# Row gathers that add in place into six accumulators, and a lasting buffer for edge offsets

## The chip, the cores and the metric

The kernel runs on one core of a Trainium2 chip. The metric is the device time of one execution in microseconds (us), as the median of several runs; lower is better. Besides the times there is one execution taken by the hardware profiler. The engines are called as the profile calls them: PE (TensorE, matmuls), DVE (VectorE), ACT (ScalarE), POOL (GpSimd, which asks for the gathers) and SP (SyncE, which asks for the plain transfers).

## The reference

A graph network with 6250 nodes, 256 channels, 100,000 edges sorted by destination, three layers and a head. Cut to what matters:

```
N, E, C, NOUT, NL = 6250, 100000, 256, 64, 4
h = relu(layernorm(x));  y = h
def agg(y): return segment_sum(y[src], dst, num_segments=N)
for l in range(NL - 1):
    t = relu((y + agg(y)) @ W1s[l] + b1s[l])
    t = relu(t @ W2s[l] + b2s[l])
    y = t @ W3s[l] + b3s[l]
t = relu((y + agg(y)) @ cW1 + cb1)
t = relu(t @ cW2 + cb2)
return x + t @ cW3 + cb3
```

All arrays are float32. Each node has some 16 incoming edges, so `agg` sums some 16 rows of 256 values per node, four times over.

## The kernel before, in words

**Blocks and two ways to aggregate.** The 6250 nodes are 49 blocks of 128. Since matrix products commute with the sum over edges, each layer's table holds rows that are multiplied by the layer's first weights already, and the aggregation works on these. Most blocks are aggregated on PE: a matrix of edge counts (uint8) is built once from one-hot tiles, kept in DRAM, and multiplied in every layer with the table, which lies in SBUF as a high and a low part (`XY`). These are the `panels`; a product step is line 1565, its operand `a` is a cast of a uint8 chunk by ACT or DVE (lines 1538 and 1540).

**Gathered blocks.** The blocks in `gone` are aggregated from rows instead (`Gathered`, lines 1341 to 1484): 22 blocks in layer 0 and 18 in each of the three others, 76 in all. For each block POOL issues 19 indirect DMAs, each of 128 rows of 1 KB, one row for each node of the block: `K` = 17 take the first 17 edges of every node (`idx`), `OV` = 2 take the block's further edges (`over`), which a small matmul with a one-hot (`hot`) sums into the right nodes. In the kernel before, the first 16 rows come in pairs into tiles `rows` of [128, 2, 256], seven of them in turn; row 17 and the two overflow gathers have tiles `last`. `pair` (lines 1413 to 1419) adds each pair of rows on DVE into `acc` as soon as it is due; `fold` (line 1421) adds the table's own rows, both halves of `acc` and row 17 into `u`, and then makes `hot`; `add` (line 1442) runs the overflow matmuls `sums` on PE; `finish` adds them into `u`, transposes and goes on to the layer's matmuls.

**What sets the order.** Everything runs under an order written out by hand: PE's stream of matmuls advances a clock (`passed`, line 1515), and the gathers of a layer are spread evenly over it. `begin` (line 1370) sets the layer's `first` and `pace`; `flow` and `send` (lines 1375 to 1398) issue each gather `LEAD` = 13 clock us ahead of its event, bound to the last matmul so far by a semaphore (`after`). `advance` runs `pair`, `fold` and `add` when their event is due, whether the rows have landed or not: an engine then waits in order at that instruction.

**Preparation.** Before the matrix is built, the edges of each block are found (`look`, from line 612): `from_i` (line 816) holds for each of the 128 nodes of the 22 gathered blocks where its run of edges begins, and 22 gathers on POOL (line 606, asked for in line 821) take 17 sources from there for each node into `idx`. `from_i` is in the preparation's pool. When that pool is closed, the build's tiles, `pairs` (line 1061) first, are laid over its memory. At build step `READY` = 22 (line 1607) `slot_rows` (line 850) masks `idx` on DVE, and layer 0's gathers begin. A build step is two one-hot matmuls (line 1108) and the cast of their result; steps run two at a time before the first product.

Of the kernel before, what the change touches and what calls it, by code (L numbers as in the profile page):

```python
# [8 lines left out]
F32 = mybir.dt.float32  # L9
I32 = mybir.dt.int32  # L10
# [4 lines left out]
OP = mybir.AluOpType  # L15
PSUM = bass.MemoryType.PSUM
DRAM = bass.MemoryType.DRAM
P = 128
# [378 lines left out]
def sorted_edges(  # L397
# [38 lines left out]
    nc = tc.nc  # L436
    N, C = x.shape
# [16 lines left out]
    K, OV = 17, 2  # L454
    SLOT = K + OV
# [14 lines left out]
    NG = sum(n for _, n in gone)  # L470
# [4 lines left out]
    const = ctx.enter_context(tc.tile_pool(name="const", bufs=1))  # L475
# [11 lines left out]
    live = const.tile([P, NG, K], F32, name="live")  # L487
    nodes3 = const.tile([P, 3, NG], F32, name="nodes3")
    gained = const.tile([P, NG], F32, name="gained")
    taken = const.tile([P, NG, 2], BF16, name="taken")  # L490
    slots = const.tile([P, OV * P], BF16, name="slots")
    kth = const.tile([P, K], F32, name="kth")
# [2 lines left out]
    colf = const.tile([P, P], F32, name="colf")  # L495
# [116 lines left out]
    def look(pool):  # L612
# [29 lines left out]
        half = pool.tile([P, 2], F32, name="half", bufs=1)  # L642
# [170 lines left out]

        st, dg = nodes3[:, 0, :], nodes3[:, 1, :]
        at0 = pool.tile([P, NG], F32, name="at0", bufs=1)
        from_i = pool.tile([P, NG], I32, name="from_i", bufs=1)
        nc.vector.tensor_scalar(at0, st, float(E - K), None, op0=OP.min)
        nc.vector.tensor_copy(from_i, at0)
        for c in range(NG):
# [177 lines left out]
    with tc.manual_schedule():  # L997
# [55 lines left out]
        hot = {}  # L1053
# [3 lines left out]
        def pair(hots, k):  # L1057

            if k < len(batches):
                s = batches[k][1]  # L1060
                pairs[s] = hots.tile([P, 2, GSUB, 2], BF16, name="pairs", bufs=3)
                nc.scalar.copy(pairs[s], clT[:, :, :, s, None].to_broadcast([P, 2, GSUB, 2]))  # L1062
# [172 lines left out]
        def bring_inputs(b0, n):  # L1235

            assert layers[NLAYER].sent == len(layers[NLAYER].order)
            assert layers[NLAYER].done == layers[NLAYER].n
            inputs[b0] = []
            for _ in range(0, n, 2):  # L1240
                t = gath.tile([P, 2, C], F32, name="rows", bufs=7)
                inputs[b0].extend((t[:, 0, :], t[:, 1, :]))
            for i, t in enumerate(inputs[b0]):
                rows_io(x, b0 + i, 1, t[:, None, :], True)
# [96 lines left out]
        class Gathered:  # L1341
            def __init__(self, l):
                self.l, self.sent, self.done = l, 0, 0
                self.first, self.turn = None, None
                self.blocks = [(b, n, i, left[q] + i)
                               for q, (b, n) in enumerate(gone) for i in range(n)
                               if l == 0 or (b, n) != panels[-1]]
                self.alone = {b + i for b, n, i, _ in self.blocks}
                self.rows, self.us, self.acc, self.hot = {}, [], None, None
                self.order = [(g, k) for g in range(len(self.blocks)) for k in range(SLOT)]  # L1350
                self.events = []
                for g in range(len(self.blocks)):
                    for k in range(3, K - 1, 2):
                        self.events.append((SLOT * g + k, lambda g=g, k=k: self.pair(g, k)))
                    self.events.append((SLOT * g + K - 1, lambda g=g: self.fold(g)))
                    self.events.append((SLOT * g + SLOT - 1, lambda g=g: self.add(g)))
                self.n = len(self.events)
# [22 lines left out]
            def send(self, upto):  # L1380
                while self.sent < min(upto, len(self.order)):
                    g, k = self.order[self.sent]
                    c = self.blocks[g][3]
                    if k < K - 1:
                        if k % 2 == 0:
                            self.rows[g, k + 1] = gath.tile([P, 2, C], F32, name="rows", bufs=7)
                        t = self.rows[g, k | 1][:, k % 2, :]
                    else:
                        t = self.rows[g, k] = gath.tile([P, C], F32, name="last", bufs=4)
                    at = idx[:, c, k:k + 1] if k < K else over[:, c, k - K:k - K + 1]  # L1390
                    got = nc.gpsimd.indirect_dma_start(  # L1391
                        out=t, out_offset=None, in_=tables[self.l][:, :],
                        in_offset=bass.IndirectOffsetOnAxis(ap=at, axis=0),
                    )
                    after(got, "rows are asked for evenly over a layer")
                    self.sent += 1
                    if self.l == 0 and k == 4 and g + 2 < len(self.blocks):
                        ahead.append(self.blocks[g + 2][3])
# [11 lines left out]
                    self.done += 1  # L1410
                    run()

            def pair(self, g, k):
                t = self.rows.pop((g, k))
                if k == 3:
                    self.acc = work.tile([P, 2, C], F32, name="acc", bufs=1)
                    nc.vector.tensor_tensor(self.acc, self.rows.pop((g, 1)), t, OP.add)
                else:
                    nc.vector.tensor_tensor(self.acc, self.acc, t, OP.add)  # L1419

            def fold(self, g):
                if self.turn in jobs:
                    jobs.remove(self.turn)
                    self.turn[2]()
                b, n, i, c = self.blocks[g]
                b += i
                u = work.tile([P, C], F32, name="u", bufs=2)
                self.us.append(u)
                nc.vector.tensor_tensor(u, XY[:, b, :C].bitcast(F32), XY[:, b, C:].bitcast(F32),  # L1429
                                        OP.add)  # L1430
                used.add((self.l, b, 0))
                if (self.l, b, 1) in used:
                    used.add((self.l, b))
                    reload(self.l, b)
                nc.vector.tensor_tensor(u, u, self.acc[:, 0, :], OP.add)  # L1435
                nc.vector.tensor_tensor(u, u, self.acc[:, 1, :], OP.add)  # L1436
                nc.vector.tensor_tensor(u, u, self.rows.pop((g, K - 1)), OP.add)
                self.hot = work.tile([P, OV, P], F32, name="hot", bufs=2)
                nc.vector.tensor_tensor(self.hot, colf[:, None, :].to_broadcast([P, OV, P]),  # L1439
                                        rel[:, c, :, None].to_broadcast([P, OV, P]), OP.is_equal)  # L1440

            def add(self, g):
                b, n, i, _ = self.blocks[g]
                for j in range(OV):
                    mm = nc.tensor.matmul(sums[:, :C], self.hot[:, j, :], self.rows.pop((g, K + j)),  # L1445
                                          start=(j == 0), stop=(j == OV - 1))
                    passed(C * FULL32, mm)
                self.finish(b, n, i, sums)
# [42 lines left out]
        units = [(0, -1, j) for j in range(PRE)] + [  # L1491
            (l, p, j) for l in range(NLAYER + 1) for p in range(last[l] + 1) for j in range(NT)]
        sums = ps_g.tile([P, W], F32, name="sums")
        LEAD, TAIL = 13.0, 10.0
        COLS, FULL32, TURN, BUILD, BURST = 0.457e-3, 1.68e-3, 0.4, 0.2, 0.3
        clock = [0.0]
        FAR, SPAN = 7, 6
# [101 lines left out]
        with tc.tile_pool(name="hots", bufs=1) as hots, tc.tile_pool(  # L1599
            name="ats", bufs=1  # L1600
        ) as ats, tc.tile_pool(name="rings", bufs=AHEAD + 2) as rings, tc.tile_pool(
            name="gath", bufs=1
        ) as gath, tc.tile_pool(
            name="ps_a", bufs=2, space=PSUM
        ) as ps_a, tc.tile_pool(name="ps_b", bufs=2, space=PSUM) as ps_b:
            begun = {0: clock[0]}
            READY = 22
            spread = {u: [] for u in range(2, 2 * PRE + 1, 2)}
            spread[READY - 4], spread[READY - 2] = [layers[0].blocks[0][3]], [
                layers[0].blocks[1][3]]  # L1610
            beside = build(hots, ats, ps_b)
            while now[0] < PRE:
                for _ in range(2):
                    next(beside)
                    built[0] += 1
                if built[0] == READY:
                    slot_rows()
                    layers[0].begin()
                for c in spread[built[0]]:
                    overflow(hots, c)  # L1620
                tick(layers[0])
                layers[0].advance()
                if built[0] == GSUB * (panels[0][1] - 1) + 4:
                    open_chunks()
            later(1, lambda: later(2, lambda bad=verdict(): judge(bad)))
            for p in range(last[0] + 1):
                product(0, p, ps_a, beside)
            assert next(beside, None) is None and built[0] == total
# [72 lines left out]
```

## Time and profile before

| what | value |
|---|---|
| median of 3 runs | 2530.39 us (2521.58 to 2542.65) |
| profiled execution | 2534.08 us, its span 2532.2 us |
| mean granted PE clock | 0.923 of full speed |
| DVE busy in pairwise adds, first and further (lines 1417, 1419) | 52.2 and 313.0 us |
| indirect DMAs on POOL, L1391 | 1216 of `rows`, 76 + 152 of `last` |
| DMA engines' mean share over the layers | 0.49 to 0.52 |

The profile gives, for each engine, the time that its instructions took, and for each group of instructions the idle time ahead of it with what ended it (`<-`). A line `A <- B: t, n, m` of the waits says that A's engine stood idle n times for t us in all, at most m us in one piece, until B was done. In a timeline row stand the start, the duration, the engine, the line, the operation with out<-in and shapes, and in brackets the idle time before it.

### The profile page before, as it was taken

The page shows a single profiled execution, that of the slowest core. Times are in us where ns is not written, and L with a number is a line of the kernel's source. Part 1 is how long each engine was busy: PE and PEld are TensorE (multiplying, and loading weights), DVE is VectorE, ACT ScalarE, POOL GpSimd, SP SyncE. Part 2 cuts the span into 40 slices and gives each one's busy share as a digit, 9 for nine tenths or more (in the row PEclk, how much of TensorE's full clock was granted, in tenths as well). Part 3 has the DMA queues.
Part 4 walks back from the last instruction along what each step waited for, and adds up shares of the span by engine and source line. Part 5 has one row for each costly group of instructions (what it writes and reads, how often), then busy time and mean ns, then how long its engine had stood idle before and what let it go on. Part 6 is the DMA issues. An engine that isn't in the chain of part 4 may idle for free. (4 is left out here: it accounts for less than half of the span.)

```text
span 2532.2 us, 29316 instructions
## 1 busy us (share of the span) xinstructions
PE 2149.9 (85%) x9093; PEld 1603.5 (63%) x9093; DVE 1315.5 (52%) x2939; ACT 896.4 (35%) x1812; POOL 1588.1 (63%) x1574
## 2 busy tenths in 40 slices
PE   5848878777787899989989899899898989888888
PEld 3726655555555687666667686666666866666665
DVE  6758666666666644444334553344334544444344
ACT  4745453434444443222223432222223422222222
POOL 3356666666666537767667367676667276777673
PEclk9959998988898899999999999999999999899898
DMA  5425545444445555444545455445445545554553
GB/s 154 137 85 168 161 136 153 148 143 150 151 136 174 171 168 150 148 148 136 157 143 155 145 178 154 148 139 157 141 156 157 166 152 166 158 160 145 169 156 106
DMA packets 201369, 381.40 MB, mean 151 GB/s; under 512 B 35538, under 2 KB 126050, under 8 KB 201204
## 3 DMA queue, kind: packets, MB, share of 16 engines
q0 software_dynamic: 72768, 192.26, 25.9%
q1 hardware_dynamic: 126510, 185.34, 22.6%
q10 hardware_dynamic: 1926, 1.85, 0.3%
q8 instruction: 73, 1.20, 0.2%
q14 instruction: 92, 0.75, 0.1%
HBM read 320.38 MB, written 58.59 MB: 150 GB/s over the span
## 5 line engine op out<-in xcount | busy, mean ns | idle before, releaser
L1565 PE MATMUL agg<-a,XY 128*128 128x512 f32 (+1 forms) x6076 | 1612.1, 415 | 121.7 <-issue 74.8
L1391 POOL DMA_INDIRECT rows<-table,idx x1216 | 1237.7, 1018 | 681.8 <-issue 220.6
L1565 PEld LDWEIGHTS agg<-a,XY 128*128 128x128 f32 x6076 | 1173.2, 200 | 418.3 <-issue 136.4
L1538 ACT CAST a<-at 128x512 fp32r<-128x512 uint8 (+1 forms) x943 | 546.3, 606 | 769.0 <-PE agg L1565 464.3
L1540 DVE CAST a<-at 128x512 fp32r<-128x512 uint8 (+1 forms) x576 | 260.3, 461 | 443.4 <-PE agg L1565 229.6
L1419 DVE TENSOR_TENSOR acc<-acc,rows 128x512 f32<-128x512 f32 x456 | 313.0, 686 | 34.2 <-DMA rows<-table,idx 23.1
L1108 PE MATMUL bp<-hi,lo 128*128 128x196 bf16 x992 | 154.9, 272 | 139.8 <-issue 49.3
L1116 ACT CAST at<-bp 128x392 uint8<-128x392 f32 x276 | 131.4, 486 | 356.3 <-PE bp L1108 157.5
L1118 DVE CAST at<-bp 128x392 uint8<-128x392 f32 x220 | 123.9, 563 | 196.1 <-PE bp L1108 98.7
L1108 PEld LDWEIGHTS <-lo 128*128 128x128 bf16 x992 | 84.9, 104 | 219.1 <-issue 155.8
L1391 POOL DMA_INDIRECT last<-table,over x152 | 159.6, 1050 | 75.4 <-issue 25.4
L1260 PE MATMUL ps<-h,w 128*128 128x512 f32 (+5 forms) x392 | 162.3, 554 | 2.2 <-issue 2.0
L1289 PE MATMUL ps<-w,h 128*128 128x256 f32 x588 | 142.2, 388 | 17.7 <-ACT h L1473 6.3
L1067 DVE TENSOR_TENSOR hi<-cols,pairs 128x784 bf16<-128x784 bf16 x248 | 139.3, 562 | 0.0
L1289 PEld LDWEIGHTS ps<-w,h 128*128 128x128 f32 x588 | 112.8, 194 | 41.3 <-issue 17.3
L1455 DVE TENSOR_TENSOR u<-u,sums 128x256 f32<-128x256 f32 x76 | 31.8, 418 | 202.3 <-PE agg L1565 161.7
L1067 DVE TENSOR_TENSOR lo<-lanes,pairs 128x512 bf16<-128x512 bf16 x248 | 104.1, 420 | 26.1 <-ACT pairs L1062 23.1
L1260 PEld LDWEIGHTS ps<-h,w 128*128 128x128 f32 (+1 forms) x392 | 68.8, 189 | 69.9 <-issue 60.6
L1445 PE MATMUL sums<-last,hot 128*128 128x256 f32 x304 | 85.7, 405 | 27.7 <-DVE hot L1439 18.1
L1263 ACT ACTIVATE h<-ps,bias 128x512 f32<-128x512 f32 (+5 forms) x98 | 60.5, 634 | 133.8 <-PE agg L1565 56.6
L1391 POOL DMA_INDIRECT last<-table,idx x76 | 80.8, 1063 | 38.6 <-issue 13.8
L1307 DVE TENSOR_TENSOR zz<-ps,w 128x512 f32<-128x512 f32 (+1 forms) x78 | 50.1, 657 | 93.7 <-PE agg L1565 36.3
(167 smaller groups left out, 1110.5 us busy)
## 6 DMA issues: line engine op xcount, KB each, us to landing
at<-mat SPq DMA_DIRECT2D x189, 448.0 KB
mat<-at SPq DMA_DIRECT2D x31, 784.0 KB
rows<-table,idx POOLq DMA_INDIRECT x1216
table<-zz SPq DMA_DIRECT2D x69, 256.0 KB
back<-table SPq DMA_DIRECT2D x118, 128.0 KB
at<-mat SPq DMA_DIRECT2D x25, 336.0 KB
xs<-in_x_dram SPq DMA_DIRECT2D x8, 768.0 KB
table<-zs SPq DMA_DIRECT2D x24, 256.0 KB
```

Of the source, the lines that this page charges most:

```text
L1067: nc.vector.tensor_tensor(o.rearrange("p q (n t) -> p q n t", t=2), values.rearrange("p (n t) -> p n t", t=2)[:, None, :, :].to_broadcast( ...
L1108: mm = nc.tensor.matmul(bp[:, m * HW:(m + 1) * HW], lo[:, q + m, :], hi[:, q + m, :], start=True, stop=True)
L1116: nc.scalar.copy(o, v)
L1118: nc.vector.tensor_copy(o, v)
L1260: mm = nc.tensor.matmul(ps[:mp, :w], weights[l][0][:, c, i * P:i * P + mp], h1[:, c, :w], start=(c == 0), stop=(c == KC - 1))
L1289: mm = nc.tensor.matmul(o, h2[0][:, c, nodes], w3[:, c, :], start=(c == 0), stop=(c == KC - 1))
L1391: got = nc.gpsimd.indirect_dma_start(out=t, out_offset=None, in_=tables[self.l][:, :], in_offset=bass.IndirectOffsetOnAxis(ap=at, axis=0),)
L1419: nc.vector.tensor_tensor(self.acc, self.acc, t, OP.add)
L1445: mm = nc.tensor.matmul(sums[:, :C], self.hot[:, j, :], self.rows.pop((g, K + j)), start=(j == 0), stop=(j == OV - 1))
L1538: nc.scalar.copy(o, mat[l, p][j])
L1540: nc.vector.tensor_copy(o, mat[l, p][j])
L1565: mm = nc.tensor.matmul(agg[c][:, :w], XY[:, j, o:o + P], a[:, :w], start=(j == 0 and half == 0), stop=(j == NT - 1 and half == 1))
```

## The change

The rows of a block no longer get tiles of their own. A block has one tile `acc` of [128, 6, 256] (`CHAINS` = 6), two of them in turn. Gather k goes into slot k mod 6: the first six are plain gathers, and the other eleven add to what lies there in the DMA itself (`compute_op`), so each waits until the gather six before it has landed. Row 17 goes this way too; only the overflow gathers keep tiles `last`. `pair` is gone. `fold` adds one half of `acc` to the other (three rows at once) and then three rows into `u`. `acc` and `hot` are kept by block, as two blocks can be open at once. `from_i` moves into the pool that lasts. `READY` goes from 22 to 50. At the end, the inputs of the last panel use two of the `acc` tiles.

```diff
+    from_i = const.tile([P, NG], I32, name="from_i")
...
-        from_i = pool.tile([P, NG], I32, name="from_i", bufs=1)
...
-                t = gath.tile([P, 2, C], F32, name="rows", bufs=7)
+                t = gath.tile([P, CHAINS, C], F32, name="acc", bufs=2)
...
-                    for k in range(3, K - 1, 2):
-                        self.events.append((SLOT * g + k, lambda g=g, k=k: self.pair(g, k)))
                     self.events.append((SLOT * g + K - 1, lambda g=g: self.fold(g)))
...
-                    if k < K - 1:
-                        if k % 2 == 0:
-                            self.rows[g, k + 1] = gath.tile([P, 2, C], F32, name="rows", bufs=7)
-                        t = self.rows[g, k | 1][:, k % 2, :]
+                    if k == 0:
+                        self.acc[g] = gath.tile([P, CHAINS, C], F32, name="acc", bufs=2)
+                    if k < K:
+                        t = self.acc[g][:, k % CHAINS, :]
                     else:
                         t = self.rows[g, k] = gath.tile([P, C], F32, name="last", bufs=4)
                     at = idx[:, c, k:k + 1] if k < K else over[:, c, k - K:k - K + 1]
                     got = nc.gpsimd.indirect_dma_start(
                         out=t, out_offset=None, in_=tables[self.l][:, :],
                         in_offset=bass.IndirectOffsetOnAxis(ap=at, axis=0),
+                        compute_op=OP.add if CHAINS <= k < K else OP.bypass,
                     )
...
-            def pair(self, g, k):
-                t = self.rows.pop((g, k))
-                if k == 3:
-                    self.acc = work.tile([P, 2, C], F32, name="acc", bufs=1)
-                    nc.vector.tensor_tensor(self.acc, self.rows.pop((g, 1)), t, OP.add)
-                else:
-                    nc.vector.tensor_tensor(self.acc, self.acc, t, OP.add)
...
-                nc.vector.tensor_tensor(u, u, self.acc[:, 0, :], OP.add)
-                nc.vector.tensor_tensor(u, u, self.acc[:, 1, :], OP.add)
-                nc.vector.tensor_tensor(u, u, self.rows.pop((g, K - 1)), OP.add)
-                self.hot = work.tile([P, OV, P], F32, name="hot", bufs=2)
-                nc.vector.tensor_tensor(self.hot, colf[:, None, :].to_broadcast([P, OV, P]),
+                acc = self.acc.pop(g)
+                half = CHAINS // 2
+                nc.vector.tensor_tensor(acc[:, :half, :], acc[:, :half, :], acc[:, half:, :],
+                                        OP.add)
+                for i in range(half):
+                    nc.vector.tensor_tensor(u, u, acc[:, i, :], OP.add)
+                self.hot[g] = work.tile([P, OV, P], F32, name="hot", bufs=2)
+                nc.vector.tensor_tensor(self.hot[g], colf[:, None, :].to_broadcast([P, OV, P]),
                                         rel[:, c, :, None].to_broadcast([P, OV, P]), OP.is_equal)
...
-        LEAD, TAIL = 13.0, 10.0
+        LEAD, TAIL, CHAINS = 13.0, 10.0, 6
...
-            READY = 22
+            READY = 50
```

More of the change, by code (lines that the diff above doesn't have):

```diff
@@ L1348, in __init__ @@
                 self.alone = {b + i for b, n, i, _ in self.blocks}
-                self.rows, self.us, self.acc, self.hot = {}, [], None, None
+                self.rows, self.us, self.acc, self.hot = {}, [], {}, {}
                 self.order = [(g, k) for g in range(len(self.blocks)) for k in range(SLOT)]
@@ L1443, in add @@
                 b, n, i, _ = self.blocks[g]
+                hot = self.hot.pop(g)
                 for j in range(OV):
-                    mm = nc.tensor.matmul(sums[:, :C], self.hot[:, j, :], self.rows.pop((g, K + j)),
+                    mm = nc.tensor.matmul(sums[:, :C], hot[:, j, :], self.rows.pop((g, K + j)),
                                           start=(j == 0), stop=(j == OV - 1))
```

## The prediction

> **What bounds the kernel now.** I read the page first (busy time by engine, DMA queues), then the waits of TensorE, then the groups by line, and last the stages of POOL, the engine that asks for the gathers.
>
> ```profile
> span 2532.2 us, 29316 instructions
> PE 2149.9 (85%) x9093; PEld 1603.5 (63%) x9093; DVE 1315.5 (52%) x2939; ACT 896.4 (35%) x1812; POOL 1588.1 (63%) x1574
> q0 software_dynamic: 72768, 192.26, 25.9%
> q1 hardware_dynamic: 126510, 185.34, 22.6%
> ```
>
> TensorE (PE) is busy for 85% and the chain of waits runs through it, so only what PE waits for can shorten the kernel. VectorE (DVE) at 52% is no bound by its sum. The DMA engines are about half used (q0 holds the gathers). The profiled run took 2534.1 us, the span and 1.9 us around it, 3.7 us over the median 2530.4; the sum below is made against 2534.1.
>
> The waits of PE after the preparation, and the largest one by itself, with the timeline around it (start, duration, engine):
>
> ```profile
> PE bp L1108 <- DVE lo L1067: 27.3, 3, 25.8
> PE sums L1445 <- DVE hot L1439: 18.1, 9, 4.5
> PE bp L1108 <- DVE at L1118: 16.0, 12, 3.1
> PE bp L1108 <- DVE hi L1067: 15.7, 19, 1.8
> PE pt L861 <- DVE hit L858: 9.0, 8, 2.9
> PE agg L1565 <- DVE a L1540: 7.1, 4, 3.1
> PE sums L1445 <- DVE u L1437: 5.2, 3, 2.8
> ...
> ACT pairs L1062 <- DMA idx<-in_src_dram,from_i: 23.3, 1, 23.3
> DVE lo L1067 <- ACT pairs L1062: 23.1, 1, 23.1
> ```
>
> ```profile
> 130.80 1.02 DVE L973 TENSOR_TENSOR XY<-zs,XY 128x512 fp32r<-128x512 f32 x2
> 130.91 0.73 SPq L518 DMA_DIRECT2D table<-zs  x2
> ...
> 152.05 0.95 POOL L606 DMA_INDIRECT idx<-in_src_dram,from_i  x1 [0.30 <-issue]
> 154.66 0.40 ACT L1062 COPY pairs<-clT 128x64 bf16<-128x64 bf16 x2 [23.33 <-DMA idx<-in_src_dram,from_i]
> ...
> 155.89 0.81 PE L1108 MATMUL bp<-hi,lo 128*128 128x196 bf16 x4 [25.78 <-DVE lo L1067]
> ...
> 156.95 0.87 PE L1108 MATMUL bp<-hi,lo 128*128 128x196 bf16 x4 [0.25 <-ACT at L1116]
> ...
> 172.35 1.05 POOL L1391 DMA_INDIRECT rows<-table,idx  x1 [0.30 <-issue]
> ```
>
> PE stands still for 25.8 us in one piece. `pairs`, the first tile of the matrix build, lies on memory that `from_i` held in the closed preparation pool, and 22 edge-run gathers still read `from_i`. They have nothing else to do with the build. The other waits that DVE ends are small pieces: 18.1 + 16.0 + 15.7 + 9.0 + 7.1 + 5.2 = 71 us.
>
> **The change part by part.**
>
> *Lasting `from_i`.* In the changed program DVE's first one-hot no longer waits on gather queues; it keeps only the SP queue's waits. The wait on the edge runs moves to `slot_rows`. What is late next is the preparation's last work: DVE ends at 130.80 + 1.02 = 131.8, and the last two stores of `zs` are issued by 130.91 + 0.73 = 131.6. If nothing follows, `pairs` starts 154.66 - 131.8 = 22.9 us earlier; if these stores land as late as the 4.0 us gather below, 154.66 - 135.6 = 19.1. I take **-21**.
>
> *READY 22 to 50.* Two build steps take 156.95 - 155.89 = 1.06 us, so the 28 steps are 15 us, and `slot_rows`, two overflow lists and the first gathers move behind them. `slot_rows` is queued on DVE ahead of the one-hots, so it must not wait. The build now starts near 134.7, step 50 comes 25 x 1.06 = 26.5 us later, at 161, and the edge runs land by 154.66, as nothing moves their issue: 6 us of cover. That cover would be gone if the 22 issues beside busy DVE took 0.3 us more each, and DVE and soon PE would stand for the excess. First rows were asked for 172.35 - 155.89 = 16.5 us into the build, now 16.5 + 15 = 31.5: at 166, 6 us earlier, while PE is 21 earlier. Layer 0's gathers lose 15 us of room. Cost on the path: 0.
>
> *Fold in place of pairwise adds.* The preparation's stage (length, then busy time of PE, its weight loads, DVE, ACT, POOL) and groups of DVE and POOL:
>
> ```profile
> 0.00:131.00 131.00, 91.15 (x445) 70.38 (x445) 93.78 (x261) 74.64 (x156) 47.56 (x69) 0.93 0.47 144
> ```
>
> ```profile
> L1391 POOL DMA_INDIRECT rows<-table,idx x1216 | 1237.7, 1018 | 681.8 <-issue 220.6 <-PE agg L1565 196.6 <-remote 56.0
> L1419 DVE TENSOR_TENSOR acc<-acc,rows 128x512 f32<-128x512 f32 x456 | 313.0, 686 | 34.2 <-DMA rows<-table,idx 23.1 <-issue 8.7 <-DVE a L1540 0.5
> L1417 DVE TENSOR_TENSOR acc<-rows 128x512 f32<-128x512 f32 x76 | 52.2, 686 | 57.3 <-DMA rows<-table,idx 41.2 <-issue 16.1
> L1435 DVE TENSOR_TENSOR u<-u,acc 128x256 f32<-128x256 f32 x76 | 32.6, 429 | 2.6
> L1436 DVE TENSOR_TENSOR u<-u,acc 128x256 f32<-128x256 f32 x76 | 32.3, 425 | 2.6
> L1437 DVE TENSOR_TENSOR u<-u,last 128x256 f32<-128x256 f32 x76 | 32.3, 425 | 3.1 <-DVE u L1436 0.5
> L606 POOL DMA_INDIRECT wd<-in_dst_dram,starts x16 | 17.0, 1062 | 15.0 <-DVE starts L703 4.3 <-remote 3.3 <-issue 2.7
> ```
>
> Removed: 313.0 + 52.2 + 32.6 + 32.3 + 32.3 = 462 us. Added per block: one add of 768 columns and three of 256. From 256 to 512 columns costs 0.686 - 0.425 = 0.261, so 768 is 0.947; with 3 x 0.425 it is 2.22, times 76 blocks 169. DVE loses 293 us, 24% of its 1315.5 - 93.8 after the preparation. It also no longer stops at a pair whose rows have not landed (23.1 + 41.2 us); the wait is only at the fold. This lies beside PE except where DVE ended a PE wait, 71 us. Lower end: 24% of them, 17. Upper end: all 71. I take **-28**, nearer the lower, since casts and one-hots, untouched, end most of them.
>
> *Block end.* The chain at a layer's end, with the ends of POOL's and DVE's part:
>
> ```profile
> 1417.84 1.03 POOL L1391 DMA_INDIRECT last<-table,idx  x1 [0.30 <-issue]
> ...
> 1422.42 0.43 DVE L1437 TENSOR_TENSOR u<-u,last 128x256 f32<-128x256 f32 x1 [0.53 <-DVE u L1436]
> 1422.76 0.42 DVE L1439 TENSOR_TENSOR hot<-colf,rel 128x256 f32<-128x256 f32 x1
> ```
>
> ```profile
> 1420.45 4.00 DMA last<-table,over
> 1424.44 0.04 issue
> 1424.49 1.22 PE sums L1445 x2
> ```
>
> A gather lands 4.0 us after its issue (1422.42 - 1417.84 = 4.6 at most for row 17). Now the whole fold waits for row 17: 0.947 + 1.275 + 0.42 for `hot` = 2.64 us after 1422.42 is 1425.1, where 1424.49 was enough: 0.6 us, plus whatever an accumulate lands later. Ends: 0.6 and, at a doubled 4.0, 4.6 us at each of 4 layers' ends. I take **+3** in all.
>
> *Eleven of 17 gathers add in place* (76 x 11 = 836; six chains, so gather k waits until k-6 has landed). No row shows an accumulate. Its POOL time lies between a plain issue, 0.957 (the median; the mean above is 1.018), and twice that, 1.91; below nothing there is no reason, as it moves the same rows and more. POOL's stages by layer (length, busy time and count, granted clock, DMA share, GB/s), one issue with its gap, and the minimum, median and maximum of an issue:
>
> ```profile
> 172.00:876.00 704.00, 473.76 (x461) 0.90 0.50 155
> 919.00:1422.00 503.00, 348.66 (x342) 0.97 0.51 157
> 1460.00:1964.00 504.00, 347.55 (x342) 0.95 0.50 154
> 2002.00:2504.00 502.00, 351.70 (x342) 0.91 0.52 159
> ```
>
> ```profile
> 1006.27 0.96 POOL L1391 DMA_INDIRECT rows<-table,idx  x1 [0.30 <-issue]
> ```
>
> ```profile
> L1391 POOL DMA_INDIRECT rows<-table,idx x1216: 951/957/1784, 172.4 to 2497.8; - x174
> ```
>
> With the 0.30 us gap per issue POOL has free 704 - 474 - 138 = 92, and 52, 54 and 48 us in the other layers; less the 15 above, 231 us. That absorbs 231 / 836 = 0.28 us per accumulate. I take 0.1 us more than plain, since a gather of 98 short rows (`wd`, 1.062) and one of 128 long ones (1.018) hardly differ, so what a descriptor holds seems to matter little: **0** on the path. Chain waits: six issues back is at least 6 x 1.26 = 7.5 us, on average 6 x 502 / 342 = 8.8, against a landing in 4.0 to (doubled) 8.0: 0. Bytes: if an accumulate takes twice the engine time, q0's 25.9% grows by 836 / 1444 of itself, 15 points, and is with q1 some 64%: no bound.
>
> Sum: 2534.1 - 21 - 28 + 3 = 2488, on the median's scale 2485.
>
> **The rule that speaks against it.** The Trainium skill, "Collectives: The Full Stack", section "The bandwidth ceiling", states that an add in the DMA path needs two source reads and two read descriptors per chunk, and halves the throughput; its "GPSIMD Engine Reference", section 4, says that one of a pair of cores emits the read descriptors. By both, an accumulate would take up to double POOL's 0.957 us; no run here shows it yet. What that would do is the first rival's upper end.
>
> **The rivals.**
>
> 1. *POOL becomes the bound: slower.* For it: the last layer's POOL has 48 of 502 us free, and each late row stops DVE at the fold, in order ahead of the casts, and so PE. Against: POOL's price hardly varies over its kinds of gather. Accumulates that cost d more give 836d - 231 us late; that eats the 46 gained at d = 277 / 836 = 0.33, an issue of 1.29 us. At half more (d = 0.48) it is 2485 + 400 - 231 = 2654, at double 3054. Chance 0.22, of which 0.06 near double. A landing over 8.8 us would do the same through the chains and is counted here.
> 2. *Only the stall goes.* PE waits that DVE ended pass to ACT, which casts as many operands, or folds that wait for the slowest chain give the relief back: 2534 - 21 + 3 = 2516, on the median's scale 2512. For it: casts, not adds, end most waits. Against: DVE also leaves 64 us of waits on rows. Chance 0.20.
> 3. *The stall stays*, because another tile of the preparation holds the place, and `slot_rows` stops DVE instead: 2534 - 28 + 3 = 2509, or 2505. Against: the changed waits name only SP's queues. Chance 0.03.
>
> **How the numbers follow.** Forecast 0.55, rivals 0.22, 0.20, 0.03. The likeliest case's own range is 2436 + 3 (all 71 us go, 22.9 of the stall: 2439) to 2500 (lower relief, 19.1, block ends 6); I use 2460 downward, as all 71 is unlikely. Rivals 2 and 3 lie inside any range up to 2520; from rival 1, d of 0.33 to 0.42 (2485 + 351 - 231 = 2605) is taken in, so 2460 to 2600 leaves some 0.18 out. Faster by over 1% (below 2505; about what a measurement here can tell from no change): the forecast and a little of rivals 2 and 3, 0.57. Within 1%: the rest of them, 0.21. Slower: 0.22.
>
> **What would show it.** Stall: the first `bp` matmul near 135 us, PE's 25.8 us wait gone, no new wait of DVE at `slot_rows`. Relief: DVE busy near 1020, waits of PE on `hot`, `at`, `hi` down by a third. POOL: the accumulates a group at 0.96 to 1.1 us; over 1.29 and the forecast is wrong. Chains: POOL waiting on its own gathers for under some us a layer. A layer end that is over 5 us later, or folds that wait long on `acc`, would show late accumulates.

## The result, and the profile after

The changed kernel takes 2767.05 us (median of 4 runs, 2765.33 to 2768.19), where the kernel before took 2533.47 us (4 runs, 2521.58 to 2542.65) beside it: a ratio of 1.0924, 95% interval 1.0876 to 1.0972. It is 9.2% slower, outside the predicted range. The profiled execution took 2767.37 us.

Its span, its engines and the two large DMA queues (packets, MB, share of 16 engines):

```profile
span 2765.6 us, 28294 instructions
PE 2129.6 (77%) x9093; PEld 1631.5 (59%) x9093; DVE 1070.0 (39%) x2483; ACT 905.1 (33%) x1812; POOL 2046.9 (74%) x1574
q0 software_dynamic: 153024, 192.26, 38.6%
q1 hardware_dynamic: 126510, 185.34, 20.9%
```

DVE lost 246 us and PE 20, yet the span grew by 233. POOL grew by 459 us with the same 1574 instructions (ACT by 9, PE's weight loads by 28). The gathers' bytes are the same 192.26 MB, but their packets more than doubled: 80,256 more, which is 96 for each of the 836 accumulating gathers.

The groups of the changed lines (busy time, mean ns; idle time ahead, and what ended it):

```profile
L1389 POOL DMA_INDIRECT acc<-table,idx x1292 | 1787.9, 1384 | 517.2 <-issue 246.4
L1440 PE MATMUL sums<-last,hot 128*128 128x256 f32 x304 | 141.1, 612 | 440.4 <-DVE hot L1433 412.2
L1428 DVE TENSOR_TENSOR acc<-acc 128x768 f32<-128x768 f32 x76 | 72.9, 959 | 741.6 <-DMA acc<-table,idx 727.7
...
L1389 POOL DMA_INDIRECT last<-table,over x152 | 149.9, 986 | 46.3 <-issue 36.6
```

The longest waits of DVE and PE on the path, and POOL's wait for landings (us in total, times, longest):

```profile
DVE acc L1428 <- DMA acc<-table,idx: 727.7, 72, 16.8
...
PE sums L1440 <- DVE hot L1433: 412.2, 58, 17.4
...
POOL acc L1389 <- DMA acc<-table,idx: 30.2, 99, 0.3
```

Read upward: PE stands 412 us at `sums` because `hot` comes late on DVE; DVE stands 728 us at the fold because the last gather into `acc` has not landed; POOL itself waits for a landing only 30.2 us, in pieces of at most 0.3. So the chains are not waited for. The rows come late because POOL cannot ask for them sooner. One block's end on POOL and the fold behind it on DVE:

```profile
1118.21 1.55 POOL L1389 DMA_INDIRECT acc<-table,idx  x1 [0.30 <-PE ps L1260]
1120.07 1.55 POOL L1389 DMA_INDIRECT acc<-table,idx  x1 [0.30 <-issue]
1121.92 1.55 POOL L1389 DMA_INDIRECT acc<-table,idx  x1 [0.30 <-issue]
1123.77 1.00 POOL L1389 DMA_INDIRECT last<-table,over  x1 [0.30 <-issue]
1125.07 0.97 POOL L1389 DMA_INDIRECT last<-table,over  x1 [0.30 <-issue]
```

```profile
1125.87 0.96 DVE L1428 TENSOR_TENSOR acc<-acc 128x768 f32<-128x768 f32 x1 [15.10 <-DMA acc<-table,idx]
```

An accumulating gather holds POOL 1.55 us where a plain one holds it 0.957. With the 0.30 us gap, issues stand 1.85 us apart instead of 1.26, so d = 0.59 us. It has landed 1125.87 - 1121.92 = 3.95 us after its issue began. The median time from the start of an issue to its landing, in the changed kernel (run e13 below, most of its gathers add) and in one whose gathers are all plain (e12):

```profile
acc<-table,idx POOLq DMA_INDIRECT x1292, 3.8
```

```profile
rows<-table,idx POOLq DMA_INDIRECT x1216, 3.0
```

That is 0.8 us later, of which POOL's own 0.59 us are the most: the price lies mainly in POOL's time, not in the transfer's. The prediction's first rival had a formula for this, 836d - 231; with 0.59 it gives 262 us, or 2485 + 262 = 2747.

The start of the matrix build, and the stage from there to the edge runs' landing (length, busy time of PE, its loads, DVE, ACT, POOL; granted clock, DMA share, GB/s):

```profile
133.27 0.50 PE L1108 MATMUL bp<-hi,lo 128*128 128x196 bf16 x4 [4.47 <-DMA idx<-in_src_dram,from_i]
```

```profile
131.00:155.00 24.00, 5.64 (x26) 3.02 (x27) 6.47 (x15) 6.02 (x15) 16.10 (x17) 0.56 0.15 36
```

The 25.8 us stall is gone as one piece: the build starts at 133.27, not 155.89. But until 155, while POOL still issues the edge-run gathers, PE works only 5.64 of 24 us. The first product starts at 182.19 where it was 190.45, 8 us earlier and not 21. This belongs to the chip: in e13, the same kernel on another chip, the build starts at 127.55, PE works three times as much in the same stretch, although POOL's edge-run gathers go on until 146, and the first product starts at 161.22:

```profile
131.00:155.00 24.00, 18.17 (x89) 9.37 (x87) 20.04 (x50) 19.32 (x49) 11.72 (x12) 0.50 0.34 101
```

### The profile page after: what moved, and what is told of

Read it like the earlier page. It is cut to its first block, busy times and chain, and to the rows that moved or that the text cites. A ratio compares the mean times of both kernels' runs of the same rounds, so it can differ in the third digit from the quotient of the medians.

```text
span 2765.6 us, 28294 instructions
## 1 busy us (share of the span) xinstructions
PE 2129.6 (77%) x9093; PEld 1631.5 (59%) x9093; DVE 1070.0 (39%) x2483; ACT 905.1 (33%) x1812; POOL 2046.9 (74%) x1574
## 3 DMA queue, kind: packets, MB, share of 16 engines
q0 software_dynamic: 153024, 192.26, 38.6%
q1 hardware_dynamic: 126510, 185.34, 20.9%
q10 hardware_dynamic: 1926, 1.85, 0.2%
## 5 line engine op out<-in xcount | busy, mean ns | idle before, releaser
L1389 POOL DMA_INDIRECT acc<-table,idx x1292 | 1787.9, 1384 | 517.2 <-issue 246.4
L1560 PE MATMUL agg<-a,XY 128*128 128x512 f32 (+1 forms) x6076 | 1565.2, 412 | 6.6 <-ACT h L1576 2.4
L1533 ACT CAST a<-at 128x512 fp32r<-128x512 uint8 (+1 forms) x943 | 553.9, 607 | 891.2 <-PE agg L1560 731.7
L1440 PE MATMUL sums<-last,hot 128*128 128x256 f32 x304 | 141.1, 612 | 440.4 <-DVE hot L1433 412.2
L1440 PEld LDWEIGHTS sums<-last,hot 128*128 128x128 f32 x304 | 82.4, 295 | 491.8 <-DVE hot L1433 444.5
L1428 DVE TENSOR_TENSOR acc<-acc 128x768 f32<-128x768 f32 x76 | 72.9, 959 | 741.6 <-DMA acc<-table,idx 727.7
L1389 POOL DMA_INDIRECT last<-table,over x152 | 149.9, 986 | 46.3 <-issue 36.6
L1431 DVE TENSOR_TENSOR u<-u,acc 128x256 f32<-128x256 f32 x228 | 97.0, 425 | 7.9
L1468 ACT ACTIVATE h<-ps,bias 128x256 f32<-128x256 f32 (+1 forms) x84 | 33.5, 450 | 154.2 <-PE ps L1461 150.7
```

The lines of the kernel that those rows point to most:

```text
L1389: got = nc.gpsimd.indirect_dma_start(out=t, out_offset=None, in_=tables[self.l][:, :], in_offset=bass.IndirectOffsetOnAxis(ap=at, axis=0), ...
L1431: nc.vector.tensor_tensor(u, u, acc[:, i, :], OP.add)
L1440: mm = nc.tensor.matmul(sums[:, :C], hot[:, j, :], self.rows.pop((g, K + j)), start=(j == 0), stop=(j == OV - 1))
L1533: nc.scalar.copy(o, mat[l, p][j])
L1560: mm = nc.tensor.matmul(agg[c][:, :w], XY[:, j, o:o + P], a[:, :w], start=(j == 0 and half == 0), stop=(j == NT - 1 and half == 1))
```

## The experiments

Theory 1: the price of an accumulating gather on POOL is the whole loss, since POOL sets the pace once its room is used up. Rivals: the chains (each add must wait for the slot's last landing); the fold, which stands for all seventeen rows and has only two `acc` tiles; the DMA engines' added reads and packets.

The runs fall on different chips, and that matters here. The first four kernels ran on a chip where the kernel before takes 2529 us, about as in the result above; the others ran on two chips where it takes 2292 to 2293. Each row is compared with the kernel before on its own chip. "Rest" is the span less POOL's busy time.

| run | what differs | time, us | before, us | ratio (95%) | POOL busy, us | rest, us |
|---|---|---|---|---|---|---|
| e1 | changed kernel, no gather adds | 2528.79 | 2528.93 | 0.9993 (0.9977 to 1.001) | 1548.9 | 978.3 |
| e2 | before, one memset behind 836 gathers | 2545.02 | 2528.93 | one run | 1883.1 | 659.8 |
| e3 | before, `from_i` and READY 50 | 2539.96 | 2528.93 | 1.0041 (1.002 to 1.0062) | 1592.4 | 938.1 |
| e4 | changed kernel, three chains | 3045.21 | 2528.93 | one run | 2163.0 | 880.3 |
| e5 | changed kernel, five of seventeen add | 2459.16 | 2293.04 | 1.0723 (1.0702 to 1.0744) | 1762.3 | 695.2 |
| e6 | changed kernel, eight chains | 2688.87 | 2293.04 | one run | 1991.6 | 695.5 |
| e7 | before, `from_i`, READY 22 | 2280.27 | 2293.04 | 0.9945 (0.9927 to 0.9962) | 1581.4 | 699.2 |
| e8 | before, fold alone, no gather adds | 2258.91 | 2293.04 | 0.9856 (0.9833 to 0.9878) | 1541.7 | 713.6 |
| e9 | before, two memsets behind 836 gathers | 2959.95 | 2292.75 | one run | 2031.9 | 925.9 |
| e10 | changed kernel, four kinds of gather | 2496.30 | 2292.75 | one run | 1795.0 | 699.4 |
| e11 | as e7 | 2278.33 | 2292.75 | 0.9936 (0.992 to 0.9952) | 1579.0 | 699.6 |
| e12 | as e3 | 2271.54 | 2292.75 | 0.9915 (0.9898 to 0.9932) | 1573.0 | 697.2 |
| e13 | the changed kernel | 2742.81 | 2292.36 | 1.1962 (1.193 to 1.1994) | 2046.0 | 696.6 |
| e14 | as e1, two memsets behind 836 gathers | 2890.85 | 2292.36 | 1.2604 (1.2573 to 1.2635) | 1929.0 | 962.6 |
| e15 | as e1 | 2246.05 | 2292.36 | 0.979 (0.9764 to 0.9815) | 1548.2 | 698.6 |

### Adding or not (e1)

```diff
-                        compute_op=OP.add if CHAINS <= k < K else OP.bypass,
+                        compute_op=OP.bypass,
```

> The changed kernel, but all 17 gathers of a block are plain: the eleven that added in place now overwrite, so eleven of seventeen rows are left out of the sums. Chains, slots, waits on the gather six before, folds and buffers stay. Theory 1 (an accumulate holds POOL some 0.59 us longer than a plain gather, 1.55 against 0.96 us, and POOL is the bound): POOL's issues go back to 0.96 us and the time to about 2490 us, 2460 to 2520. Theory 2 (the chains' waits for the gather six before are the cost) and theory 3 (the fold that waits for all rows of a block, with two tiles in turn): the time stays near 2767 us.

Without the adding the loss is gone, with the chains, the fold and the buffers kept. So with plain gathers neither chains nor fold have a measurable share, and POOL's 30.2 us above say that with adding ones the chains do not wait either. Against expectation there was also no gain: 0.9993, although the stall was gone and DVE 252 us lighter. What POOL had free can be read here from its own idle time:

```profile
span 2527.2 us, 28294 instructions
L1389 POOL DMA_INDIRECT acc<-table,idx x1292 | 1286.5, 996 | 732.3 <-issue 247.3
...
L1389 POOL DMA_INDIRECT last<-table,over x152 | 150.1, 988 | 90.4 <-PE agg L1560 34.4
```

POOL idles 732.3 us ahead of these gathers, where the changed kernel shows 517.2: 215 us were free, and 90.4 - 46.3 = 44 more ahead of the `last` gathers, 259 in all. The measured loss is 836 x 0.59 = 493 less that, 234; the two spans differ by 238.

### A POOL that is held, with no transfer added (e2, e9, e14)

```diff
                     after(got, "rows are asked for evenly over a layer")
+                    if 6 <= k < K:
+                        nc.gpsimd.memset(idle, 0.0)
+                        nc.gpsimd.memset(idle[:, :160], 0.0)
```

e2 has the first memset only, in the kernel before; e9 both, in the kernel before; e14 both, the second of 16 columns, in the kernel of e1.

> The kernel before, with a useless memset of 128x256 on POOL behind eleven of the seventeen gathers of each block, 836 in all; nothing else changed, no DMA adds anything. Theory 1: POOL time alone does it. If a memset holds POOL for p us with its gap, the time is about 2533 + 836 p - 245 (the room that POOL had before): 2533 to 2560 at p = 0.3, 2700 at p = 0.5, 2780 at p = 0.59. Rival (the DMA engines, which are 0.60 busy in the changed kernel against 0.49, slow the gathers and the other transfers down): about 2533 us whatever p is, since no DMA changes.

> The kernel before, nothing changed but POOL: two memsets of idle memory (128x256, 0.35 us in the second kernel run here, and 128x160, about 0.24) behind eleven of seventeen gathers, 836 times, so that POOL is held about as long as by the change's accumulating gathers (0.59 us each, 493 us in all), with no transfer added and none of them adding. In the runs so far the span less POOL's busy time is 695 us where POOL never waits for long (five and nine accumulating gathers a block, 695.2 and 695.5), 660 with one memset. Theory 1 (POOL's time, wherever it goes): POOL busy 1588 + 493 = 2081 us, the span 2741 to 2776 us, whatever the chip's time for the kernel before. Rival (the added reads and packets of the transfers): no more than 2570 us, since no packet is added.

> The changed kernel with all gathers overwriting (eleven of seventeen rows are missing from the sums) and two memsets of idle memory on POOL (128x256 and 128x16) behind each gather of rows 6 to 16, so that its pitch on POOL is about that of an accumulating gather, 1.85 us: 0.96 + 0.34 + 0.05 + 0.05 + 0.47 = 1.87 us by the rows of the earlier filler. It has the plain gathers' packets and no chain. Theory 1 (POOL's time alone): the time of the changed kernel on this chip, within 1%, or above it by 836 x 0.02 = 17 us. Rival (the packets, reads or chains have a share): below the changed kernel by that share, 50 us or more.

e2 fell inside its range for a short memset (2533 to 2560 us), which lies so near the rival's 2533 that it decides nothing. The times expected for e9 and e14 were missed: for e9 I summed the memsets' durations and not the distance from gather to gather, and for e14 I took the small memset at 0.05 us and the gap behind it at 0.47, where the rows below show 0.11 and 0.59. The timelines of e2, e9 and e14 in this order:

```profile
1119.57 0.34 POOL L1398 MEMSET idle<- 128x256 f32 x1
1120.07 0.97 POOL L1392 DMA_INDIRECT rows<-table,idx  x1 [0.16 <-issue]
1121.04 0.33 POOL L1398 MEMSET idle<- 128x256 f32 x1
1121.53 0.97 POOL L1392 DMA_INDIRECT rows<-table,idx  x1 [0.16 <-issue]
```

```profile
1119.95 0.96 POOL L1392 DMA_INDIRECT rows<-table,idx  x1 [0.49 <-PE agg L1569]
1120.91 0.33 POOL L1398 MEMSET idle<- 128x256 f32 x1
1121.29 0.23 POOL L1399 MEMSET idle<- 128x160 f32 x1
1121.99 0.96 POOL L1392 DMA_INDIRECT rows<-table,idx  x1 [0.47 <-issue]
```

```profile
1114.46 0.96 POOL L1390 DMA_INDIRECT acc<-table,idx  x1 [0.59 <-issue]
1115.42 0.33 POOL L1397 MEMSET idle<- 128x256 f32 x1
1115.81 0.11 POOL L1398 MEMSET idle<- 128x16 f32 x1
1116.51 0.96 POOL L1390 DMA_INDIRECT acc<-table,idx  x1 [0.59 <-PE agg L1564]
```

One memset takes up part of the issue gap: 1.46 us from gather to gather instead of 1.26. With two it is 2.04 to 2.05, whether the second has 160 columns or 16. By these distances the times come out. e2: 836 x 0.20 = 167 us, within the 259 us of room, and it cost only 16 (a single run). e9: 836 x 0.79 = 660 us, measured 2959.95 - 2292.75 = 667. e14 against e15 on one chip: the same 660, measured 2891.6 - 2246.8 = 645. The changed kernel against e15 on that chip: 836 x 0.59 = 493, measured 2742.6 - 2246.8 = 496. The memsets add no packet to the gathers and no row of the sums hangs on them, yet each microsecond of distance costs nearly the same. So POOL's time suffices for the whole loss, and the added reads and packets need no share.

### How many add (e5, e6, e4)

```diff
-                        compute_op=OP.add if CHAINS <= k < K else OP.bypass,
+                        compute_op=OP.add if CHAINS <= k < CHAINS + 5 else OP.bypass,
```

That is e5; e6 has CHAINS = 8 and e4 has CHAINS = 3, with all rows summed.

> The changed kernel with only the gathers of rows 6 to 10 of each block adding in place; those of rows 11 to 16 overwrite (so six of seventeen rows are missing from the sums). 76 x 5 = 380 accumulating gathers are left. Theory 1 (POOL's time: an accumulating gather occupies POOL 0.59 us longer, and the first 231 to 276 us of that are absorbed by POOL's idle time): 380 x 0.59 = 224 us, all absorbed, so 2529 us as without any, at most 2540. Rival (each accumulating gather costs the same wherever it stands, as a transfer that is late: 238 us / 836 = 0.285 us each): 2529 + 380 x 0.285 = 2637 us.

> The changed kernel with eight chains: rows 8 to 16 add, nine a block, 684 accumulating gathers, the whole sum as in the reference; fold is one add of 128x1024 and four of 256. Theory 1 (POOL's time beyond a room of about 255 us): 684 x 0.59 - 255 = 149 us over 2529, so about 2678 us. Rival (the same cost for each accumulating gather, 0.285 us): 2529 + 684 x 0.285 = 2724 us. Rival (the chains are waited for, not POOL): hardly below 2767 us, since a longer fold is added and a chain still has two adds in turn.

> The changed kernel with three accumulators instead of six: 14 of 17 gathers of a block add in place, each waiting for the gather three before. Theory 1: three more accumulates a block, 76 x 3 x 0.59 = 134 us more, 2900 us, with POOL busy almost all the time. Theory 2: the chains' waits become long (three issues of 1.85 us are 5.5 us, and a landing takes about 4 us), POOL stands waiting for its own gathers, and the time is well over 2900 us, 3100 or more.

e5 took 2459, not 2529 or 2637: both numbers were for the first chip. From e15 it is 211 us up for 380 x 0.59 = 224, so on this chip there is hardly any room. e6 came out at 2689 for 2678, which is partly luck: without room, its 684 x 0.59 = 404 us on e15's 2246 would be 2650; its POOL is busy 443 us more than e15's, 0.65 us for each adding gather. Taken row by row, 0.58 of that are the adding gathers' own; the rest lies in plain ones, above all the first of each block, right behind the adding gathers (1.39 us on average, 1.06 in e15). The table shows the firmer reading: on these two chips, in every kernel without memsets, whatever else it changes, the span is POOL's busy time and 695 to 714 us. From e5 to e6 POOL's busy time rises by 229.3 us and the span by 229.6. The changed kernel itself came out as this says, 2742.81 us (e13) where 2742 to 2767 were expected: within 25 us of its time on the first chip, although the kernel before differs by 237 us between the two.

With three chains the waits do appear, on top of the price (e4, its gathers and their wait for landings):

```profile
L1389 POOL DMA_INDIRECT acc<-table,idx x1292 | 1901.4, 1472 | 686.4 <-issue 223.4
POOL acc L1389 <- DMA acc<-table,idx: 157.5, 201, 4.1
```

Theory 1 alone had 2900 us, its rival 3100 or more; 3045 lies between. POOL is busy 116 us more than in the changed kernel and idle 169 more ahead of these gathers; the span is 278 longer. Six chains were enough to keep landings out of the way, three are not.

### The price by itself (e10)

```diff
+                    if CHAINS <= k < K and k % 4 > 1:
+                        t, at = t[:64], at[:64]
...
+                    elif CHAINS <= k < K and k % 4 == 2:
+                        got = nc.gpsimd.indirect_dma_start(out=t, out_offset=None, in_=tables[self.l][:, :], in_offset=by, compute_op=OP.add)
...
```

> The price of an accumulating gather by itself. The changed kernel with rows 6 to 16 of each block asked for in four ways on four lines: rows 8, 12 and 16 add, 128 rows of the table; 9 and 13 overwrite, 128 rows; 6, 10 and 14 add, only 64 rows (partitions 0 to 63); 7, 11 and 15 overwrite, 64 rows. (Rows that overwrite or halve are missing from the sums.) If the price is by row: 1.55, 0.96, about 0.8 and about 0.5 us, 0.59 to 0.3 the surcharge. If it is a fixed cost of the instruction: the surcharge of 64 rows is 0.59 as well. POOL's work comes out as without any adding gather, so the time does too: 0.98 to 1.00 of before on the same chip.

```profile
L1399 POOL DMA_INDIRECT acc<-table,idx x608 | 629.3, 1035 | 310.2 <-issue 114.9 <-ACT a L1539 43.0 <-DMA cw<-in_L_gnn_cW_dram 41.3
L1393 POOL DMA_INDIRECT acc<-table,idx x228 | 357.3, 1567 | 69.5 <-issue 33.2 <-PE agg L1566 24.1 <-PE bp L1108 3.4
L1395 POOL DMA_INDIRECT acc<-table,idx x228 | 333.6, 1463 | 69.5 <-issue 32.9 <-PE agg L1566 25.9 <-PE bp L1108 4.3
L1397 POOL DMA_INDIRECT acc<-table,idx x228 | 217.0, 952 | 69.5 <-PE agg L1566 24.1 <-DMA acc<-table,idx 24.1 <-issue 13.1
```

In this order: plain and adding with 128 rows, adding and plain with 64. The first line is a mixture: it also holds the first six gathers of each block, some of them slowed by the adding ones ahead. Its gathers 9 and 13, which stand among the other kinds, have a mean of 1.01 us in the trace. So half the rows save 0.10 us when adding and 0.06 when plain, and the surcharge is 0.56 us with 128 rows and 0.51 with 64: it belongs to the instruction, and hardly to its rows. The time missed its expectation (1.089 of before, not 0.98 to 1.00) because the halved gathers save so little: POOL's busy time is 1795.0, and with the usual rest of about 699 that is the span of 2494.4.

### The other two parts alone (e3, e7, e11, e12, e8, e15)

```diff
+    from_i = const.tile([P, NG], I32, name="from_i")
-        from_i = pool.tile([P, NG], I32, name="from_i", bufs=1)
-            READY = 22
+            READY = 50
```

e7 and e11 are without the last two lines; e8 has the new tiles and the fold but neither of these edits.

> The kernel before with the lasting buffer for the edge offsets and READY = 50 alone. By the prediction's first step 21 us less, 2512 us. By the changed kernel's trace, where the build starts 22 us earlier but its casts then come slowly until the edge-run gathers have landed, and the first product comes only 8 us earlier: 2525 us.

> The kernel before with only the lasting from_i; READY stays at 22. If the 25.8 us stall at the edge runs' offsets is worth its length to the end, 2505 to 2512 us. If it is READY = 50 that gave the gain back (the third kernel run here, with both, took 2540 us, 1.0041 of before), this one is below before: under 2515 us. If the layers' spacing takes the gain back whatever READY is, within 0.3% of before: 2522 to 2538 us.

> The kernel before with only the new buffers and the fold, all seventeen gathers overwriting (eleven of seventeen rows are missing from the sums), from_i and READY as before. It takes the 293 us of pairwise adds from VectorE and nothing else. The prediction's step: 28 us less than before, 17 to 71 (2500 us). From the run with everything but the accumulation (2529 us) less the run with from_i and READY alone (2540 us): 11 us less, about 2518 us. If VectorE's time is covered altogether: 2530 us, within 0.2% of before.

> The kernel before with the lasting from_i alone, READY 22, again, to stand beside READY 50 on one chip (it took 0.9945 of before in the runs where before took 2293 us). Where before takes about 2290 us: 0.994 again. Where before takes about 2530 us: 0.99 to 1.00 if READY takes the gain back, 1.004 if READY has no part in it.

> The kernel before with the lasting from_i and READY 50 (1.0041 of before where before took 2529 us). If READY 50 costs: 0.3 to 1% above the run with READY 22 on this chip. If it does not: within 0.2% of it.

> The changed kernel with all gathers overwriting, without the filler (eleven of seventeen rows are missing from the sums). 0.98 to 0.99 of before where before takes 2293 us (the fold alone took 0.9856, from_i with READY 50 alone 0.9915: 0.977 if the two add up); 0.9993 of before where before takes 2530 us, as in the first of these runs.

> The changed kernel itself, beside the next two on one chip. Theory 1 (POOL's time): POOL busy 2047 us and 695 to 719 us beside it, so 2742 to 2767 us on any chip: 1.19 to 1.21 of before where before takes 2293 us, 1.09 where it takes 2530 us.

On the two chips with 2293 us, the parts pay about as forecast: `from_i` and READY 50 take 21.2 us off (e12), the fold 34.1 (e8), both 46.3 (e15), so that they do not quite add up. READY 50 costs nothing there; e12 is 7 us below e11, though their intervals overlap a little. The traces show why it helps: with READY 22 the masks of `slot_rows` come before the edge runs have landed and DVE stands (e11), with READY 50 it does not, and the first product starts at 161.73 (e12) instead of 172.37 us.

```profile
151.09 0.63 DVE L852 SCALAR_TENSOR_TENSOR live<-idx,pad,live 128x374 f32<-128x374 int32 x1 [7.41 <-DMA idx<-in_src_dram,from_i]
```

On the chip with 2529 us, `from_i` and READY 50 cost 0.4%, where both expectations (2512 and 2525 us) had a gain, and the whole change without the adding gives nothing. Of the kernels that compute the whole sum, the one with `from_i` and READY 50 is the fastest on the other two chips (0.9915 of before); on the first chip it is the kernel before (1.0041).

The same kernel on both kinds of chip, first where it takes 2540 us (e3), then where it takes 2272 (e12), the aggregation's matmuls on PE and the casts for them on DVE:

```profile
span 2530.5 us, 29308 instructions
L1565 PE MATMUL agg<-a,XY 128*128 128x512 f32 (+1 forms) x6076 | 1592.6, 411 | 119.3 <-issue 90.0
L1540 DVE CAST a<-at 128x512 fp32r<-128x512 uint8 (+1 forms) x576 | 262.8, 466 | 406.2 <-PE agg L1565 251.3
```

```profile
span 2270.2 us, 29308 instructions
L1565 PE MATMUL agg<-a,XY 128*128 128x512 f32 (+1 forms) x6076 | 1517.6, 402 | 19.8 <-DVE a L1540 15.0
L1540 DVE CAST a<-at 128x512 fp32r<-128x512 uint8 (+1 forms) x576 | 249.9, 450 | 23.5 <-PE agg L1565 20.0
```

On the first chip PE's matmuls carry 75 us more busy time and 90 us of idle time that ends in nothing the trace shows, and DVE idles behind PE. The build has such stops too; in e3 they are 201 us over all of PE's matmuls, and in e12 there is none:

```profile
PE agg L1565 <- issue: 90.0, 139, 7.0
PE bp L1108 <- issue: 70.2, 52, 5.5
```

That POOL has room on the first chip is measured (e2). That PE paces the kernel there is read from these rows and no run tests it; nor does one show where the stops come from. On the second PE runs dense, and each microsecond more on POOL is one more in the span (e5, e6): the kernel has shrunk onto POOL's line (1573.0 + 697.2).

## Why the prediction was wrong, by its own steps

*Eleven of 17 gathers add in place*: this step failed, and with it the sum. It put an accumulating gather 0.1 us above a plain one, since gathers of few short and of many long rows "hardly differ, so what a descriptor holds seems to matter little". The observation holds (e10: half the rows, 0.06 to 0.10 us). The inference does not: rows that vary only in number and length say nothing about another kind of operation. Measured, d is 0.59 us: 1.55 lies between 0.957 and 1.91 nearer to the middle than to either end, and 836 x 0.59 = 493 us went beyond POOL's room by 234, where the step put 0 on the path. The midpoint of the step's own bounds, 1.43, would have given 836 x 0.48 - 231 = 170 us late. The Trainium skill, "Collectives: The Full Stack", section "The bandwidth ceiling", says of a ReduceScatter that its add needs two read descriptors per chunk, where a copy needs one, and that this halves its throughput. The trace agrees in direction (96 more packets for each adding gather), but POOL pays 1.6 times and not double, and mostly by the instruction.

*POOL's room of 231 us*: right where it was read (259 in e1's idle time; the loss came out 238). It is no property of the kernel, though. On the chips with 2293 us it is nearly nil (e5: 13 us), and the same change costs 19.6%.

*First rival*: this is what happened, with the place, the formula and the point of decision (0.33) as stated. Its 2747 for d = 0.59 is only 20 us under 2767 in part by luck: the sum under it still counted 46 us of gains that this chip did not give, and its room was 28 us too small. Its chance of 0.22 was too low beside a term whose ends were a factor of two apart and whose room ended near a third of the way.

*Lasting `from_i`*, -21: the stall went, but on the first chip not its time (e3: 1.0041). The first product comes earlier (176.76 in e3, 182.19 in the changed kernel, 190.45 before), yet in e3 the gathers of layer 1 begin at 914.08 where it was 919.72, and those of layer 2 at 1461.36 where it was 1460.98. On the other chips the step is right in size, 21.2 us (e12), and the first product comes 22 us earlier (160.69 in e15, 183.16 in e8). What takes the gain back on the first chip is not settled.

*READY 22 to 50*, 0: right as far as it went. `slot_rows` did not wait, and with READY 22 it would have (7.41 us in e11).

*Fold in place of pairwise adds*, -28: DVE's relief was right in its first part (the groups give 462 - 72.9 - 97.0 = 292 us less where 293 were forecast, though the engine's total fell only 246), and worth 11 us on the first chip (e1 against e3) and 34 on another (e8). Not by the mechanism named, though. On that chip the kernel goes by POOL's line, and with the fold POOL is busy 1541.7 us where it was 1581.4 in e7: its plain issues have a mean of 0.995 instead of 1.018 us. That lighter DVE work shortens POOL's issues is only argued from this; e7 also differs from e8 in `from_i`, and no run isolates it.

*Block end*, +3: not measured by itself; the folds' 728 us of waiting cover it. *Chain waits*, 0, and *bytes*, no bound: right (30.2 us in pieces of 0.3; queue shares 38.6 and 20.9%, 60% together where 64 was estimated).

## What to carry to other kernels

Price an operation that no row shows by both ends and ask how far the room reaches into that interval; a nearby row that varies something else is no reason to take the cheap end. When work moves into a DMA, count what the issuing engine pays: here 246 us off a DVE with time to spare were bought with 459 us on POOL, which had some 250 at best. And for an engine that issues back to back, sum the distance from one issue to the next, gap included, not the durations. A room that was read off one chip may be gone on another.

## What the runs showed of the hardware

- An accumulating indirect gather holds POOL 1.55 us, a plain one 0.957 (128 rows of 1 KB). The surcharge is nearly the same with 64 rows (0.51 against 0.56 us, e10). It moves 96 packets more, and the median landing comes 3.8 us after the start of the issue instead of 3.0 (e13, e12).
- POOL's 0.30 us between two indirect DMAs is partly filled by other work: one memset of 0.33 us moves the next gather only 0.20 us. A second memset of 0.11 or 0.23 us moves it by 0.58 to 0.59 more, in either size.
- The same kernel took 2529 us on one chip and 2292 to 2293 on two others, and POOL's room went with that: 167 us more on POOL cost 16 us on the first (e2), 224 us cost 211 on another (e5). Mean granted clocks were 0.931 and 0.953 for one kernel (e3, e12), and PE's stops without a cause in the trace 201 us and none. The cause of the difference was not found.
- On the first chip, while POOL issued the 22 edge-run gathers at the start, PE, DVE and ACT did the matrix build's first steps at a fraction of their usual pace (5.64 us of PE in 24 in the changed kernel). On another chip they did not (18.17 us, e13), so it is not the gathers alone; what held them the trace does not name.
